# A graph-attention kernel on one Trainium2 core: gains ahead of rank weights, earlier statistics, split last tile, and half of the first gathers beside a fetch

## The chip, the cores and the metric

The kernel runs on one core of one Trainium2 chip. The metric is the time of one execution on the device, in microseconds (us). A core has a matrix engine (TensorE, PE in the profile, with its weight loads as PEld), a vector engine (VectorE, DVE), an activation engine (ScalarE, ACT), a general engine (GpSimd, POOL) and a queue engine that issues transfers (SyncE, SP). Each takes its instructions in the order in which the program gives them, and waits for the others by semaphores. SBUF is the on-chip memory; PSUM holds what TensorE writes.

## The reference

Each of 32 images x[b] has 512 channels and 1024 nodes. Two layers follow each other; each adds its input to its output and normalises over the nodes.

```python
# layer 0: attention over the nodes, in float32
q = jnp.einsum('c,bcn->bn', wq, x)
k = jnp.einsum('c,bcn->bn', wk, x)
scores = q[:, None, :] + k[:, :, None]
scores = jnp.where(scores > 0, scores, 0.01 * scores)
att = jax.nn.softmax(scores, axis=-1)
agg = jnp.einsum('bcn,bmn->bcm', x, att)
out = jax.nn.relu(jnp.einsum('oc,bcm->bom', adj, agg) + bm[None, :, None])
x = layernorm(x + out, axis=-1)
# layer 1: a masked product
W = adj * adj
x = layernorm(x + jnp.einsum('bnf,nm->bmf', x, W) + bias, axis=-1)
```

## The kernel before

**The method.** A score is a leaky ReLU of q[n] + k[m]. Above the threshold its exponential is a product of a factor of n and a factor of m, and below it another such product. So if the nodes are sorted by q, the attention of row m is a prefix sum up to a rank plus a sum from that rank on. The kernel never forms the 1024 x 1024 matrix. For an image b it goes through these stages, which are helper functions:

- `project` (L213): TensorE makes z = x^T [wq, adj^T, wk] for 128 nodes at a time (eight steps per image, each in two parts), and ScalarE copies it to `zrow` (L229).
- `spread`, `place`, `send` (L233 to L280): q is spread over all partitions, VectorE counts each node's rank (L262), and GpSimd scatters the rows of `zrow` to DRAM in rank order (L271), into one of two buffers `td` (image number modulo 2).
- `count` (L292): ScalarE counts, by a sign with an accumulated sum (L296), how many q lie above each node's threshold; `share` (L300) makes from it the index `idx` of the table row and a few exponentials.
- `fetch` (L317): SP reads the sorted rows back into the SBUF tile `zs`, in eight transfers, 2.1 MB. Columns 0, 1, 7 and 8 of its nine come first.
- `weigh` (L334): exponentials of q (ScalarE, L344) times a triangle (VectorE, L349) make the rank weights `lw`; part 0 covers the columns that come first, part 1 the rest.
- `table` (L356), nine steps per image: TensorE multiplies two columns of `zs` by the weights (L363), ScalarE copies the sums out of PSUM to `ts` (L368), the last sum is carried into the next columns (one row copied on GpSimd or VectorE, L372, and one on ScalarE, L374), and SP writes `ts` to `td` (L377). So each step waits for the one before it. There are two buffers for `ts` and one PSUM tile for all tables (pool `ps_t`).
- `pick` (L381): GpSimd gathers (L386), for 128 nodes at a time, three rows of the table (own row, sum from above, sum from below, 6 KB together) into the tile `g`; eight gathers per image, 6.3 MB. They wait until all nine steps of the image's table are in DRAM. `g` has one buffer for all images.
- `own`, `norm` (together `shares`, L395 to L425): the weights of those three rows, for four of the eight node blocks at a time. `scale` (ScalarE, L432) and `gain` (VectorE, two operations per block, L440) add the three rows up.
- `turn` (L474): TensorE turns the result round (L478), ScalarE applies bias and relu (L482). `join` (L485): VectorE adds x and takes the statistics (`stats`, L449, L451); `root` (GpSimd, L457, L458), `shift` (VectorE, L464) and `apply` (ScalarE, L470) normalise.
- `layer1` (L494): TensorE multiplies by W + I (L500); `stats1` (VectorE, L515, L449) takes the sum with the bias out of PSUM and its statistics; `root`, `shift`, `apply` normalise and `store` (L519) writes the tile out. An image has four such tiles `mt`. The pool `ps_mm` has three PSUM tiles of 128 x 1024, shared by all large products.

**The order.** The whole order of work is written by hand: an engine runs its instructions as the program emits them, and nothing is moved by a scheduler. `begin` (L549) projects images 0, 1 and 2 and makes the table of image 0; `opening` (L606) finishes layer 0 and most of layer 1 of image 0 and brings image 1 to its gains; `slot` (L649) runs for images 1 to 29 and overlaps four images; `end` (L732) has the last two images, 30 (`s`) and 31 (`mid`), and the last tiles of 29 (`old`). `last` (L522) is the very last output tile: it goes through PSUM in two halves so that VectorE can begin on the first.

In `begin`'s third loop (L573) TensorE projects image 2 while the remaining steps of image 0's table run; at z = 3 the sorted rows of image 1 are fetched, at z = 6 all eight gathers of image 0 are emitted behind step 0 of image 1's table, and steps 3 to 8 of that table follow in `opening`, with their carried rows copied by VectorE.

In `end`, image 30's layer 0 runs together with image 31's table: two steps ahead of the turns, four in the turns and three between the first matmuls of layer 1. Then the gathers of image 31 are issued and its gains follow, with the statistics of image 30's tiles 1 and 2 between them.

Of the kernel before, what the change touches and what calls it, by code (L numbers as in the profile page):

```python
# [8 lines left out]
F32 = mybir.dt.float32  # L9
# [14 lines left out]
def gat_gcn_resnorm_kernel(  # L24
# [38 lines left out]
    nc = tc.nc  # L63
# [222 lines left out]
    def top(b):  # L286

        qs, kc, sgn, qmax = info[b]
        nc.vector.tensor_reduce(qmax, qs, AX.X, ALU.max)
        nc.vector.tensor_scalar(bws[b], nel, qmax, None, ALU.mult)  # L290
# [200 lines left out]
        if ot > 0:  # L491
            apply(0, b, ot - 1)

    def layer1(b, mt, h, cts=range(CT)):  # L494

        yt = ys[b]
        if (b, mt) not in ops:
            ops[b, mt] = ps_mm.tile([P, N], F32, name=f"o1_{b}_{mt}", tag="mm")
        for ct in cts:
            nc.tensor.matmul(  # L500
                ops[b, mt][:, h * H : (h + 1) * H],
                w1[:, ct, mt * P : (mt + 1) * P],
                yt[ct][:, h * H : (h + 1) * H],
                start=(ct == 0),
                stop=(ct == CT - 1),
            )

    def layer1g(b, mts, ct):
        for mt in mts:
            for h in range(NH):  # L510
                layer1(b, mt, h, (ct,))
# [10 lines left out]
    def last(b, mt):  # L522

        t = vpool.tile([P, N], F32, name=f"v_{b}_{mt}", tag="v")
        st = small.tile([P, NH, 6], F32, name=f"st_1_{b}_{mt}", tag="st")
        mv = small.tile([P, 2], F32, name=f"mv_1_{b}_{mt}", tag="mv")
        halves = [slice(h * H, (h + 1) * H) for h in range(NH)]
        for h, some in enumerate(halves):
            layer1(b, mt, h)
            op = ops[b, mt]  # L530
            nc.vector.tensor_tensor(t[:, some], op[:, some], bias_bc[:, some], ALU.add)
            nc.vector.bn_stats(st[:, h, :], t[:, some])
            if h == 0:
                shift(1, b, mt - 1)
                apply(1, b, mt - 1)
                store(b, mt - 1)
        nc.vector.bn_aggr(mv, st)
        due[1, b, mt] = [t, mv]
        root(1, b, mt)
        shift(1, b, mt)  # L540
        t, mv, rs, nb = due.pop((1, b, mt))
        nc.scalar.activation(t[:, halves[0]], t[:, halves[0]], AF.Identity, bias=nb, scale=rs)
        nc.vector.tensor_scalar(
            t[:, halves[1]], t[:, halves[1]], rs, nb, ALU.mult, ALU.add
        )
        for some in halves:
            nc.sync.dma_start(out=out[b, mt * P : (mt + 1) * P, some], in_=t[:, some])

    def begin():  # L549


        for z in range(NT):
            project(0, z, 0)
            project(0, z, 1)
        spread(0)
        for nt in range(NT):
            order(0, nt)
        top(0)
        fetch(0)
        for z in range(NT):  # L560
            if z == NT - 2:
                weigh(0, 0)
            if z == NT - 1:
                weigh(0, 1)
            project(1, z, 0)
            if z == NT - 1:
                table(0, 0)
            project(1, z, 1)
            count(0, z)
        table(0, 1)  # L570
        share(0)
        spread(1)
        for z in range(NT):  # L573
            step = 2 * z + 2
            for nt in range(2 * z, 2 * z + 2):
                if nt < NT:
                    place(1, nt)
            project(2, z, 0)
            if step < NB:
                table(0, step)  # L580
            if z < NT // 2:
                send(1, 2 * z)
            project(2, z, 1)
            if step + 1 < NB:
                table(0, step + 1)
            if z < NT // 2:
                send(1, 2 * z + 1)
            if z == NT // 2 - 1:
                top(1)
                fetch(1)  # L590
            if z >= NT // 2 - 1:
                for nt in range(2 * z - 6, min(2 * z - 4, NT)):
                    count(1, nt)
            if z == NT - 3:
                weigh(1, 0)
            if z == NT - 2:
                table(1, 0)
                for mt in range(NT):
                    pick(0, mt)
                weigh(1, 1)  # L600
        table(1, 1, nc.vector)
        spread(2)
        table(1, 2, nc.vector)
        share(1)

    def opening():  # L606

        for step in (3, 4):
            table(1, step, nc.vector)
        shares(0, 0, NT // 2)  # L610
        for k in range(NT // 2):
            scale(0, [k])
            gain(0, [k])
            if k % 2:
                table(1, 5 + k // 2, nc.vector)
        shares(0, NT // 2, NT)
        for k in range(NT // 2, NT):
            scale(0, [k])
            gain(0, [k])
            if k % 2:  # L620
                table(1, 5 + k // 2, nc.vector)
        for ot in range(CT):
            turn(0, ot)
            join(0, ot)
            root(0, 0, ot)
            load(3, ot)
        shift(0, 0, CT - 1)
        apply(0, 0, CT - 1)
        for mt in range(NT):
            pick(1, mt)  # L630
        for nt in range(NT):
            order(2, nt)
            count(2, nt)
        top(2)
        fetch(2)
        for ct in range(CT):
            layer1g(0, range(CT - 1), ct)
        for mt in range(CT - 1):
            stats1(0, mt)
            root(1, 0, mt)  # L640
        for ct in range(CT):
            layer1g(0, (CT - 1,), ct)
        for mt in range(CT - 1):
            shift(1, 0, mt)
        shares(1, 0, NT // 2)
        scale(1, range(NT // 2))
        gain(1, range(NT // 2))
# [84 lines left out]
    def end():  # L732

        s, mid, old = B - 2, B - 1, B - 3
        for mt in range(CT - 1):
            apply(1, old, mt)
        shares(s, NT // 2, NT)
        scale(s, range(NT // 2, NT))
        weigh(mid, 0)
        gain(s, (4, 5))  # L740
        table(mid, 0)
        weigh(mid, 1)
        gain(s, (6, 7))
        table(mid, 1)
        stats1(old, CT - 1)
        root(1, old, CT - 1)
        for ot in range(CT):
            turn(s, ot)
            table(mid, 2 + ot)
            join(s, ot)  # L750
            root(0, s, ot)
            if ot == 0:
                shift(1, old, CT - 1)
                apply(1, old, CT - 1, by=nc.vector)
        share(mid)
        shift(0, s, CT - 1)
        apply(0, s, CT - 1)
        for mt in range(CT):
            store(old, mt)
        step = 2 + CT  # L760
        for ct in range(CT):
            for mt in range(CT - 1):
                layer1g(s, (mt,), ct)
                if step < NB:
                    table(mid, step)
                    step += 1
        for mt in range(NT):
            pick(mid, mt)
        stats1(s, 0)
        root(1, s, 0)  # L770
        for ct in range(CT):
            layer1g(s, (CT - 1,), ct)
        shares(mid, 0, NT // 2)
        scale(mid, range(NT // 2))
        gain(mid, (0, 1))
        own(mid, NT // 2, NT)
        gain(mid, (2, 3))
        norm(mid, NT // 2, NT)
        scale(mid, range(NT // 2, NT))
        shift(1, s, 0)  # L780
        apply(1, s, 0)
        stats1(s, 1)
        root(1, s, 1)
        gain(mid, (4, 5))
        stats1(s, 2)
        root(1, s, 2)
        gain(mid, (6, 7))
        for mt in (1, 2):
            shift(1, s, mt)
            apply(1, s, mt)  # L790
        for ot in range(CT):
            turn(mid, ot)
            join(mid, ot)
            root(0, mid, ot)
            if ot == 0:
                stats1(s, CT - 1)
                root(1, s, CT - 1)
        shift(0, mid, CT - 1)
        apply(0, mid, CT - 1)
        shift(1, s, CT - 1)  # L800
        apply(1, s, CT - 1)
        for mt in range(CT):
            store(s, mt)
        for ct in range(CT):
            layer1g(mid, range(CT - 1), ct)
        for mt in range(CT - 1):
            stats1(mid, mt)
            root(1, mid, mt)
            if mt > 0:
                shift(1, mid, mt - 1)  # L810
                apply(1, mid, mt - 1)
                store(mid, mt - 1)
        last(mid, CT - 1)
# [35 lines left out]
```

## Time and profile before

| what | us |
|---|---|
| median of 3 runs (lowest, highest) | 2413.76 (2410.81, 2415.1) |
| the profiled execution's own time | 2413.43 |
| its span, first to last instruction | 2411.7 |
| TensorE busy | 2302.5 |
| VectorE busy | 1672.2 |
| ScalarE busy | 1439.6 |
| GpSimd busy | 1022.5 |

A line of the page's table of slices gives one digit for each of 40 equal parts of the span (60.3 us each): tenths of busy time, or tenths of the full clock in the row PEclk. A timeline line gives start, duration, engine, source line, operation, output and inputs with their shapes, and in brackets the idle time before it and what ended it. The chain of waits that ended last goes through TensorE for 69% of the span; 7% each are VectorE and the issue of instructions, 6% GpSimd and 5% transfers.

### The profile page before, as it was taken

To read this page: it belongs to the slowest core of one execution; us is meant where nothing else is said; L and a number is where in the kernel's file an instruction comes from. 1 tells how busy PE (TensorE), PEld (TensorE's weight loads), DVE (VectorE), ACT (ScalarE), POOL (GpSimd) and SP (SyncE) were. 2 spreads that over 40 slices of the span, in tenths; PEclk is the share of its full clock that TensorE was granted. 3 is DMA by queue.
4 is the path that set the end of the run, shared out by engine and by line. 5 is a ranking of instruction groups with operands and counts; after the bars stand their busy time and mean duration, and the time that the engine had idled before them with its cause. 6 is when DMAs were issued, how large, how long until landed. Compare 5 with 4: busy or idle time off the path is not lost.

```text
span 2411.7 us, 30916 instructions
## 1 busy us (share of the span) xinstructions
PE 2302.5 (95%) x9744; PEld 1449.9 (60%) x9744; DVE 1672.2 (69%) x3490; ACT 1439.6 (60%) x2213; POOL 1022.5 (42%) x1284
## 2 busy tenths in 40 slices
PE   8968999999999999999999999999999999999776
PEld 7635655666666566666566666656665656666333
DVE  3266777776777776777777677767677776768655
ACT  2555655775665666655677565566665566656532
POOL 1233445433444533444543444453344454344431
PEclk9989999999999999999999999999999999999887
DMA  6566776767777766777676777676777767677641
GB/s 240 145 229 205 251 246 235 233 211 240 256 249 234 253 213 221 250 252 233 242 231 214 243 254 254 232 247 203 233 248 254 236 244 226 212 248 243 203 177 61
DMA packets 176835, 548.67 MB, mean 228 GB/s; under 512 B 26304, under 2 KB 26304, under 8 KB 176672
## 3 DMA queue, kind: packets, MB, share of 16 engines
q1 hardware_dynamic: 117600, 276.65, 38.8%
q0 software_dynamic: 57344, 269.52, 29.4%
q8 instruction: 77, 1.26, 0.2%
q14 instruction: 86, 0.70, 0.1%
q10 hardware_dynamic: 1728, 0.53, 0.1%
HBM read 338.17 MB, written 208.43 MB: 227 GB/s over the span
## 4 chain that ended last, share of the span: by engine, by line
PE 69%; DVE 7%; issue 7%; POOL 6%; DMA 5%; ACT 4%; SPq 0%; POOLq 0%; DVEq 0%; ACTq 0%
PE zp L221 29%; PE o L500 25%; PE tp L363 10%; DVE g L440 3%; PE op L478 3%; DMA g<-td,idx 3%; POOL td L271 2%; POOL zs L372 2%; ACT y L482 1%; DVE st L449 1%; PE qb L237 1%; POOL g L386 1%; POOL rs L458 1%; ACT ts L368 1%; ACT w L344 1%
## 5 line engine op out<-in xcount | busy, mean ns | idle before, releaser
L221 PE MATMUL zp<-wmT,x 128*128 128x257 f32 x4096 | 963.0, 386 | 3.6 <-ACT zrow L229 2.6
L500 PE MATMUL o<-y,adj_sb 128*128 128x512 f32 x2048 | 897.9, 596 | 11.1 <-ACT y L470 6.1
L221 PEld LDWEIGHTS zp<-wmT,x 128*128 128x128 f32 x4096 | 761.6, 191 | 200.5 <-issue 92.9
L500 PEld LDWEIGHTS o<-y,adj_sb 128*128 128x128 f32 x2048 | 385.3, 191 | 487.2 <-issue 468.9
L372 POOL COPY zs<-ts 1x513 f32<-1x513 f32 x249 | 200.4, 805 | 657.6 <-ACT ts L368 657.4
L440 DVE SCALAR_TENSOR_TENSOR g<-g,ra 128x512 f32<-128x512 f32 x512 | 369.9, 748 | 35.1 <-ACT g L432 26.0
L363 PE MATMUL tp<-zs,lw 128*64 128x257 f32 x2304 | 325.1, 401 | 45.0 <-POOL zs L372 19.0
L271 POOL DMA_INDIRECT td<-zrow,ranki x256 | 283.5, 1108 | 195.6 <-DVE ranki L266 124.1
L229 ACT COPY zrow<-zp 128x514 f32<-128x514 f32 x256 | 148.8, 581 | 323.7 <-PE zp L221 313.1
L262 DVE SCALAR_TENSOR_TENSOR lt<-qs,zrow,first 128x1024 int8<-128x1024 f32 x256 | 326.8, 1276 | 3.6 <-ACT qs L241 2.2
L386 POOL DMA_INDIRECT g<-td,idx x256 | 268.0, 1047 | 88.1 <-issue 82.7
L296 ACT ACTIVATE sg<-qs,kc 128x1024 int8<-128x1024 f32 x256 | 294.1, 1149 | 7.0
L489 DVE TENSOR_TENSOR y<-y,x 128x1024 f32<-128x1024 f32 x128 | 156.8, 1225 | 157.9 <-ACT y L482 156.2
L363 PEld LDWEIGHTS tp<-zs,lw 128*64 128x64 f32 x2304 | 150.5, 139 | 188.1 <-POOL zs L372 57.6
L457 POOL TENSOR_SCALAR rs<-mv 128x1 f32<-128x1 f32 x256 | 81.1, 317 | 416.7 <-ACT v L470 295.0
L368 ACT COPY ts<-tp 128x514 f32<-128x514 f32 x288 | 168.6, 585 | 113.4 <-PE tp L363 107.2
L408 ACT ACTIVATE ac<-s 128x4 f32<-128x4 f32 x64 | 13.3, 208 | 358.4 <-DVE s L407 180.1
L432 ACT ACTIVATE g<-g,ra 128x512 f32<-128x512 f32 x256 | 167.3, 713 | 57.7 <-DVE ra L419 36.9
L458 POOL TENSOR_TENSOR rs<-rs,mhalf 128x1 f32<-128x1 f32 x256 | 188.8, 738 | 21.3
L464 DVE SCALAR_TENSOR_TENSOR nb<-mv,rs 128x1 f32<-128x1 f32 x256 | 39.5, 156 | 218.9 <-POOL rs L458 218.9
L515 DVE TENSOR_TENSOR v<-o,bias_bc 128x1024 f32<-128x1024 f32 x127 | 154.7, 1218 | 28.3 <-PE o L500 28.1
L478 PE MATMUL op<-ident,g 128*128 128x128 f32 x1024 | 145.4, 285 | 29.3 <-DVE g L440 17.4
(75 smaller groups left out, 1628.4 us busy)
## 6 DMA issues: line engine op xcount, KB each, us to landing
x<-in_x_dram SPq DMA_DIRECT2D x128, 512.0 KB
out_dram<-v SPq DMA_DIRECT2D x127, 512.0 KB
td<-ts SPq DMA_DIRECT2D x512, 120.5 KB
zs<-td SPq DMA_DIRECT2D x64, 602.3 KB
zs<-td SPq DMA_DIRECT2D x64, 240.9 KB
zs<-td SPq DMA_DIRECT2D x96, 120.5 KB
td<-ts SPq DMA_DIRECT2D x64, 96.4 KB
td<-zs SPq DMA_DIRECT2D x8, 514.0 KB
```

The costliest lines, as they stand in the source:

```text
L221: nc.tensor.matmul(zp[:, h, 0:CE], xb[ct][:, nt * P : (nt + 1) * P], wmT[:, ct, h * CE : (h + 1) * CE], start=(ct == 0), stop=(ct == CT - 1),)
L262: nc.vector.scalar_tensor_tensor(lt, qs, zrow[:, nt, 0:1], first[:, o : o + N], ALU.subtract, ALU.is_lt, accum_out=rank[:, nt : nt + 1],)
L271: sc = nc.gpsimd.indirect_dma_start(out=td[:, :], out_offset=bass.IndirectOffsetOnAxis(ap=ranki[:, nt : nt + 1], axis=0), in_=zrow[:, nt, ...
L296: nc.scalar.activation(sg, qs, AF.Sign, bias=kc[:, nt : nt + 1], accum_out=sgn[:, nt : nt + 1])
L363: nc.tensor.matmul(tp[i * G : (i + 1) * G, h, 0:CE], lt[:, i, j, :], zs[:, j, h * CE : (h + 1) * CE], start=True, stop=True,)
L368: nc.scalar.copy(ts.rearrange("p (h c) -> p h c", h=2), tp[:, :, 0:CE])
L372: by.tensor_copy(zs[0:1, to, 1:ZW], ts[0:1, 1:ZW])
L386: nc.gpsimd.indirect_dma_start(out=gs[b][:, mt, :], out_offset=None, in_=tds[b].rearrange("(s u) c -> s (u c)", u=3), in_offset=bass.Indir ...
L440: nc.vector.scalar_tensor_tensor(u, g[:, k, i, 1 : C + 1], ra[:, k, i : i + 1], u, ALU.mult, ALU.add)
L458: nc.gpsimd.tensor_tensor(rs, rs, mhalf, ALU.pow)
L478: nc.tensor.transpose(op[:, mt * P : (mt + 1) * P], ub[mt][:, ot * P : (ot + 1) * P], ident)
L500: nc.tensor.matmul(ops[b, mt][:, h * H : (h + 1) * H], w1[:, ct, mt * P : (mt + 1) * P], yt[ct][:, h * H : (h + 1) * H], start=(ct == 0), ...
```

## The change

In `end`, image 30's second four gains come ahead of all of image 31's rank weights. All of image 31's table steps move two places later: four in the turns, five between the matmuls, and the second part of the weights follows the second step. The statistics of image 30's tiles 0, 1 and 2 come together behind the issue of image 31's gathers, and their applies ahead of image 31's shares. In `last`, the two halves get a PSUM tile each, one from `ps_t` and one from `ps_mm`, and all of the matmuls are emitted ahead of VectorE's work. In `begin`, four of image 0's eight gathers are emitted at z = 3, ahead of image 1's fetch; the weights and steps of image 1's table move one step of the loop earlier, with the other four gathers behind step 0. Step 2 goes ahead of image 2's spread. Steps 3 to 6 stay between the gains, their carried rows copied by GpSimd; steps 7 and 8 go to the turns, and `share` of image 1 comes between the gains.

```diff
@@ layer1
-    def layer1(b, mt, h, cts=range(CT)):
+    def layer1(b, mt, h, cts=range(CT), op=None):
-        if (b, mt) not in ops:
+        if op is not None:
+            ops[b, mt] = op
+        elif (b, mt) not in ops:
@@ last
+        ops_last = (
+            ps_t.tile([P, N], F32, name="last_0", tag="t"),
+            ps_mm.tile([P, N], F32, name="last_1", tag="mm"),
+        )
+        for h in range(NH):
+            layer1(b, mt, h, op=ops_last[h])
         for h, some in enumerate(halves):
-            layer1(b, mt, h)
-            op = ops[b, mt]
+            op = ops_last[h]
@@ begin
             if z == NT // 2 - 1:
+                for mt in range(NT // 2):
+                    pick(0, mt)
                 top(1)
                 fetch(1)
...
+            if z == NT - 4:
+                weigh(1, 0)
             if z == NT - 3:
-                weigh(1, 0)
-            if z == NT - 2:
                 table(1, 0)
-                for mt in range(NT):
+                for mt in range(NT // 2, NT):
                     pick(0, mt)
                 weigh(1, 1)
-        table(1, 1, nc.vector)
+            if z == NT - 2:
+                table(1, 1, nc.vector)
+        table(1, 2, nc.vector)
         spread(2)
-        table(1, 2, nc.vector)
-        share(1)
@@ opening
-        for step in (3, 4):
-            table(1, step, nc.vector)
         shares(0, 0, NT // 2)
         for k in range(NT // 2):
             scale(0, [k])
             gain(0, [k])
             if k % 2:
-                table(1, 5 + k // 2, nc.vector)
+                table(1, 3 + k // 2)
+        share(1)
         shares(0, NT // 2, NT)
         for k in range(NT // 2, NT):
             scale(0, [k])
             gain(0, [k])
             if k % 2:
-                table(1, 5 + k // 2, nc.vector)
+                table(1, 3 + k // 2)
         for ot in range(CT):
             turn(0, ot)
+            if ot < NB - 7:
+                table(1, 7 + ot)
             join(0, ot)
@@ end
         scale(s, range(NT // 2, NT))
+        gain(s, range(NT // 2, NT))
         weigh(mid, 0)
-        gain(s, (4, 5))
-        table(mid, 0)
-        weigh(mid, 1)
-        gain(s, (6, 7))
-        table(mid, 1)
         stats1(old, CT - 1)
         root(1, old, CT - 1)
         for ot in range(CT):
             turn(s, ot)
-            table(mid, 2 + ot)
+            table(mid, ot)
+            if ot == 1:
+                weigh(mid, 1)
             join(s, ot)
...
-        step = 2 + CT
+        step = CT
         for ct in range(CT):
             for mt in range(CT - 1):
                 layer1g(s, (mt,), ct)
...
         for mt in range(NT):
             pick(mid, mt)
-        stats1(s, 0)
-        root(1, s, 0)
+        for mt in range(CT - 1):
+            stats1(s, mt)
+            root(1, s, mt)
         for ct in range(CT):
             layer1g(s, (CT - 1,), ct)
+        for mt in range(CT - 1):
+            shift(1, s, mt)
+            apply(1, s, mt)
         shares(mid, 0, NT // 2)
         scale(mid, range(NT // 2))
         gain(mid, (0, 1))
...
         scale(mid, range(NT // 2, NT))
-        shift(1, s, 0)
-        apply(1, s, 0)
-        stats1(s, 1)
-        root(1, s, 1)
-        gain(mid, (4, 5))
-        stats1(s, 2)
-        root(1, s, 2)
-        gain(mid, (6, 7))
-        for mt in (1, 2):
-            shift(1, s, mt)
-            apply(1, s, mt)
+        gain(mid, range(NT // 2, NT))
```

## The prediction

> **What bounds the kernel now.** I read the table of slices first, then the chain that ended last at the start and at the end, then the timelines of each engine there.
>
> ```profile
> PE   8968999999999999999999999999999999999776
> PEclk9989999999999999999999999999999999999887
> ```
>
> TensorE is full in 34 of 40 slices, and the change leaves these slots alone: what they begin late or early is handed on unchanged. The holes are slices 3 (120 to 180 us) and the last three (2231 on). There the chain is one of waits, so a change is worth what it moves on that chain.
>
> The opening, ScalarE, GpSimd and VectorE in the timeline (start, duration, idle before and its releaser):
>
> ```profile
> 117.72 0.60 POOL L372 COPY zs<-ts 1x513 f32<-1x513 f32 x1 [13.82 <-ACT ts L368]
> 118.33 0.69 ACT L344 ACTIVATE w<-zs,bw,el 128x7 f32<-128x7 f32 x2
> 118.83 1.51 POOL L386 DMA_INDIRECT g<-td,idx  x1 [0.51 <-issue]
> 127.38 0.59 ACT L368 COPY ts<-tp 128x514 f32<-128x514 f32 x1 [2.38 <-DMA td<-ts]
> 130.93 0.59 ACT L368 COPY ts<-tp 128x514 f32<-128x514 f32 x1 [2.32 <-DMA td<-ts]
> 132.55 0.16 DVE L405 TENSOR_TENSOR s<-g,kc 128x4 f32<-128x4 f32 x1 [0.52 <-DMA g<-td,idx]
> ```
>
> GpSimd is idle 13.8 us before the eight gathers; VectorE then waits for their first half until 132.5. The fetch of image 1's rows was issued from 106.36 to 109.70. In windows of 2 us:
>
> ```profile
> 110.00:112.00 2.00, 2.00 (x11) 1.75 (x10) 0.00 (x0) 1.52 (x4) 0.00 (x0) 1.00 1.00 274
> 130.00:132.00 2.00, 0.32 (x2) 0.00 (x0) 0.38 (x1) 1.04 (x2) 0.00 (x0) 0.50 1.01 418
> ```
>
> The last two columns are DMA share and GB/s: the fetch alone fills the DMA engines at some 240 GB/s (2 KB packets), the gathers at some 420 (6 KB).
>
> The end:
>
> ```profile
> 2290.79 1.22 DVE L515 TENSOR_TENSOR v<-o,bias_bc 128x1024 f32<-128x1024 f32 x1
> 2316.02 0.59 ACT L368 COPY ts<-tp 128x514 f32<-128x514 f32 x1 [1.74 <-PE tp L363]
> 2328.18 1.22 DVE L515 TENSOR_TENSOR v<-o,bias_bc 128x1024 f32<-128x1024 f32 x1 [18.74 <-PE o L500]
> 2341.06 0.16 DVE L405 TENSOR_TENSOR s<-g,kc 128x4 f32<-128x4 f32 x1 [2.14 <-DMA g<-td,idx]
> 2356.51 2.37 ACT L470 ACTIVATE v<-v,nb,rs 128x1024 f32<-128x1024 f32 x2 [7.56 <-DVE nb L464]
> 2358.79 2.09 ACT L482 ACTIVATE y<-op,bm_sb 128x1024 f32<-128x1024 f32 x2
> 2395.57 5.35 PE L500 MATMUL o<-y,adj_sb 128*128 128x512 f32 x8 [2.14 <-DVE v L531]
> 2400.95 0.69 DVE L531 TENSOR_TENSOR v<-o,bias_bc 128x512 f32<-128x512 f32 x1 [4.65 <-PE o L500]
> ```
>
> VectorE is idle for 18.7 us up to 2328.18, and later does two older statistics between the gains; the two older applies stand on ScalarE ahead of the first relu (2358.79); the last half's matmuls wait 2.14 us for VectorE and then run at a low clock.
>
> [...] table 1's two writes (240 KB, ready at 121.1) landed at 127.4 under the gathers, table 2's at 130.9; 240 KB in the 3.5 us between is some 65 GB/s for the SP queue. [...] idle from 2338.4, the clock is at 0.5 by 2342; but the 2.14 us at 2393.4 were enough too (0.50 from 2396 to 2398). 8 table matmuls take 1.09 us warm and 2.0 cold.
>
> **The change part by part.** The order of each engine's instructions in the new program is known; durations are the trace's.
>
> *E1, gains ahead of rank weights.* ScalarE's four scales start at 2275.48 as before; eight gains of 0.735 follow each other to 2282.1 (before, the second four ended at 2290.87, behind the large weights product of 2286.45). Small product 0.57, older statistics 2.78: 2285.4. The first turn and relu are ready by 2283.8, so join 0 runs 2285.4 to 2288.2 (before from 2293.48). Table 0: TensorE 2.25 cold, copy 0.6, then GpSimd's zs copy, queued behind the older root (1.7), ends 2287.85. Table 1 and its ScalarE copies: 2291.2; weights part 1 0.69 and the product 1.16 now stand ahead of join 1: 2293.1, VectorE idle for 2.7 us. Joins 1 to 3 then go at the old beat of 4.0 (a root lies between): the last ends at 2304.0, its apply at 2306.4 (before 2310.7).
>
> *E2, five tables instead of three behind it.* Steps 4 to 8 lie between the matmuls; the copy of step 4 is queued behind that apply on ScalarE (to 2307.0). Each further step costs a table, 1.02, plus four matmuls, 1.91: 2.93. Steps 5 to 8 reach TensorE at 2307.65, 2310.6, 2313.5, 2316.5; the last copy ends at 2318.2, 1.6 later than now (2316.6). The gathers start at 2322.6 and land at 2335.0 and 2342.6 (now 2333.4, 2341.0). So 4.3 us won upstream become 1.6 lost here.
>
> *E3, older statistics in the hole.* With table 8 done at 2317.6, TensorE finishes the three tiles after five, six and seven more groups of four matmuls (1.74; 52 took 22.59): 2326.3, 2328.1 and 2329.9; three statistics of 2.7 end at 2334.5. Their roots wait on GpSimd behind the gathers' issue (to 2332.9): last root 2335.6. ScalarE applies three (3.5): 2338.3, and the exponent of the shares stands behind them, so the scales start at 2339.4, not 2335.2. Gains 0 to 3 with the second shares: to 2346.65; norm 0.7; a scale that is no longer hidden, 0.85; four pairs, 5.9: 2354.1. Now it is 2356.4, then 2.4 of applies. New: transpose 0.5, relu at 2354.7 against 2358.79: **4.05 won**. All behind it is the same chain (join 0, statistics 3, joins) to the last tile.
>
> *E4, last halves in own buffers.* The second half's 8 matmuls follow at once at the warm rate, 8 x 0.434 = 3.5, instead of 2.14 + 5.35. In old times VectorE can start the second half at 2396.95, not 2400.95; it is free at 2396.3. **4.0 won**; aggregate, root, applies, stores and the 6.2 from the last issue to the end stay. ps_t is free by then, and the mm buffer was read at 2387.8.
>
> *O, opening.* The first four gathers start when the last table's write has landed (about 105.8 and 1.2 of issue: 107), their data 2.4 later (as at 118.83: 121.2), at 109.4. By then the fetch has moved 0.4 of its 2.1 MB. The gathers' 3.16 MB take 10.5 us beside 65 GB/s of fetch: to 119.9. The fetch's first 0.74 MB then land at about 116 (now by 113.6), the rest, 1.0 MB at 240, at about 125.6 (now by 118.3). ScalarE waits from 110.2 for the first weights, with zrow copies and signs behind, and TensorE waits at table 0 (image 1), idle about 6 us. First table's copy at about 121; the second four gathers are queued behind it on GpSimd, 122.2 (now 124.6). ScalarE waits again for part 1: to 126.3; then zrow 0.5, two signs 2.6, table copy 0.6, zs copy 0.6, zrow 0.6, table 2 on TensorE 1.1, copies 1.2, qs 1.0, and only then the shares of image 0: 134.1, gains from about 136.2 (now 134.96). So although the gathered rows are there at 121, the chain runs through the fetch. The gains drop VectorE's zs copies (0.34 net each) and take the five small operations of share (0.9): nothing net. In the turns two tables are added before the second and third turn, 2.0 each cold; VectorE's joins (beat 3.9) cover them, barely. **Cost 1.2**, unknown from both sides: below, -4.5 if the fetch keeps half of the DMA engines (part 1 at 119.5); above, +5 if its tail meets the second gathers (0.3 MB at 65). I take 1.2 because table writes were just so slow under gathers.
>
> Sum against the profiled execution's own 2413.43 (span 2411.7, 1.7 around it): - 4.05 - 4.0 + 1.2 = -6.85: **2406.6**. The median of the runs, 2413.76, is 0.3 higher.
>
> **The rivals.** *Fetch unharmed:* the opening wins 4.5, total -12.5: 2400.9. For it: the fetch starts 3 us ahead. Against: the two late table writes. *Tail collision:* opening +5, total -3: 2410.4. For it: second gathers' data at 124.6 against the fetch's end at 124.1, half a microsecond apart. *Slower:* the fetch's tail is held until both sets of gathers are through, and with it image 1's table writes. 1.7 MB at 240 is 7.1, eight gathers at 430 are 14.7: from 109.4 to 131.2, and with start gaps and landing 135; part 1 is then 9.5 late, and tables that wait for their buffers' writes add 4: +13.5, total +5.5: 2418.9. It decides from a part 1 at about 133, where the end's 8 are used up. Against: a write did land under load in 6 us, not 12. That E1 does nothing is true in a sense (E2 gives it back), and is in the sum.
>
> **How the numbers follow.** Forecast 0.56 (own range 2404 to 2409), unharmed 0.16, collision 0.20, slower 0.08. The measurement tells 0.2%, 4.8 us, from no change: the line is 2408.9. Faster: 0.50 of the forecast and 0.16, 0.66; same: 0.06 and 0.20, 0.26; slower 0.08. Range 2401.0 to 2411.5: it reaches to the collision and to the edge of the unharmed case.
>
> **What would show it.** E4: no idle before the last 8 matmuls, about 3.5 us long. E3: three statistics before the shares, no apply just ahead of the first relu of the last image. E2: last table copy 1 to 2 us later. O: ScalarE waiting for zs twice between 110 and 126, first gains near 136. I am wrong if the weights of part 1 start before 122 or after 129, or if the gathers of the last image start after 2325.

## The result

The changed kernel takes 2405.19 us (median of 7 runs, 2403.2 to 2408.18) beside 2412.61 of the kernel before (7 runs taken with them, 2406.87 to 2417.57). The ratio is 0.9973, with a 95% interval of 0.9959 to 0.9986: 6.5 us less, between 3.4 and 9.9. The profiled execution of the changed kernel is the slowest of its seven, 2408.18, with a span of 2406.5 (before: 2413.43, span 2411.7): what it shows of single stretches is one draw, and further profiles are set beside it below.

Its page, TensorE and its clock in the 40 slices (now 60.2 us each):

```profile
PE   8778999999999999999999999999999999999876
PEclk9988999999999999999999999999999999999987
```

The holes are those of before, and slice 2 (60 to 120 us) has fallen from 9 to 7. To see which part gave what, the span is cut at four instructions that every version has. *Opening:* from SP's first fetch issue for image 1 (L324) to VectorE's first later copy of `qs` (L241), when the pipeline takes over. *Slots:* from there to the last copy of `qs`, 28 turns of the loop. *Hole:* from the second shares of image 30 (L405) to the first relu of image 31 (L482). *Tail:* from there to the end.

| us | opening | slots | hole | tail | span |
|---|---|---|---|---|---|
| before | 136.93 | 1998.35 | 84.97 | 52.91 | 2411.7 |
| after | 140.79 | 1994.64 | 83.83 | 48.20 | 2406.5 |
| difference | +3.9 | -3.7 | -1.1 | -4.7 | -5.2 |
| predicted | +1.2 | 0 | -4.05 | -4.0 | -6.85 |

(The four differences make -5.7; the other half microsecond lies ahead of, between and in the cuts.) So in these two profiles the total came out near, while of the four parts only the tail did.

**The opening.** The timeline of after (start, duration, in brackets the idle time before and its releaser):

```profile
107.26 1.05 POOL L386 DMA_INDIRECT g<-td,idx  x1 [2.47 <-DMA td<-ts]
120.42 0.67 ACT L344 ACTIVATE w<-zs,bw,el 128x2 f32<-128x2 f32 x2 [9.28 <-DMA zs<-td]
121.19 2.25 PE L363 MATMUL tp<-zs,lw 128*64 128x257 f32 x8 [9.61 <-DVE lw L349]
125.28 1.02 POOL L386 DMA_INDIRECT g<-td,idx  x1 [0.17 <-issue]
128.83 0.69 ACT L344 ACTIVATE w<-zs,bw,el 128x7 f32<-128x7 f32 x2 [3.74 <-DMA zs<-td]
138.89 6.47 DVE L440 SCALAR_TENSOR_TENSOR g<-g,ra 128x512 f32<-128x512 f32 x8 [0.79 <-ACT g L432]
```

The first four gathers are issued from 107.26, as early as the fetch (issued from 107.25). ScalarE waits 9.3 us for the fetch's first part and TensorE as long behind it; the second part arrives at 128.8, after the second gathers have been issued from 125.28. The gains begin at 138.89, 3.9 later than in the profile before; 0.9 of that is the later start of the fetch (107.25 for 106.36).

The chain of waits of after, and two windows (start and end in us, then busy time by engine, granted clock, DMA share, GB/s):

```profile
109.26 10.98 DMA zs<-td
```

```profile
112.00:114.00 2.00, 0.00 (x0) 0.00 (x0) 0.00 (x0) 0.00 (x0) 0.22 (x1) 1.00 1.03 259
124.00:126.00 2.00, 2.00 (x6) 1.63 (x5) 0.00 (x0) 1.06 (x2) 1.32 (x2) 0.50 0.98 209
```

From the last fetch issue the chain does nothing but wait for that fetch. In the first window the only busy time is 0.22 us of a gather's issue on GpSimd, and the DMA engines are full. In the second they are still full with the fetch's rest.

**The end.** The timeline of after:

```profile
2308.04 1.79 PE L363 MATMUL tp<-zs,lw 128*64 128x257 f32 x8 [2.94 <-POOL zs L372]
2309.76 2.93 PE L502 MATMUL o<-y,adj_sb 128*128 128x512 f32 x4
2312.62 1.09 PE L363 MATMUL tp<-zs,lw 128*64 128x257 f32 x8
2319.67 0.59 ACT L368 COPY ts<-tp 128x514 f32<-128x514 f32 x1 [1.70 <-PE tp L363]
2323.94 1.17 POOL L386 DMA_INDIRECT g<-td,idx  x1 [5.96 <-issue]
2333.20 0.99 POOL L386 DMA_INDIRECT g<-td,idx  x1 [0.30 <-issue]
2336.56 3.50 ACT L470 ACTIVATE v<-v,nb,rs 128x1024 f32<-128x1024 f32 x3 [16.30 <-DVE nb L464]
2337.83 2.59 SPq L522 DMA_DIRECT2D out_dram<-v  x3
2346.88 0.16 DVE L405 TENSOR_TENSOR s<-g,kc 128x4 f32<-128x4 f32 x1 [2.12 <-DMA g<-td,idx]
2358.30 1.12 ACT L482 ACTIVATE y<-op,bm_sb 128x1024 f32<-128x1024 f32 x1 [4.66 <-PE op L478]
2388.65 7.03 PE L502 MATMUL last<-y,adj_sb 128*128 128x512 f32 x16
2395.71 0.69 DVE L538 TENSOR_TENSOR v<-last,bias_bc 128x512 f32<-128x512 f32 x1 [0.61 <-PE last L502]
```

The timeline of before, its last gather's issue and its stores:

```profile
2330.24 0.99 POOL L386 DMA_INDIRECT g<-td,idx  x1 [0.30 <-issue]
2348.97 49.01 SPq L520 DMA_DIRECT2D out_dram<-v  x7
```

Three things are to be seen. The last table copy (2319.67) and with it the gathers are later. The three older applies start at 2336.56, and 1.3 us later SP issues three stores of finished tiles (before, the stores began at 2348.97); the gathers' second half lands at 2346.88, 13.7 us after the last gather's issue (before: 2330.24 to 2341.06, 10.8). And the last tile's 16 matmuls run without a gap, so VectorE takes its second half at once.

The DMA view of after, 2318 to 2350 (transfers issued, KB each, median us to landing):

```profile
out_dram<-v SPq DMA_DIRECT2D x3, 512.0 KB, 8.0
g<-td,idx POOLq DMA_INDIRECT x8, 9.0
```

### The profile page after: what moved, and what is told of

The parts are those of the page before. It is cut to its first block, busy times and chain, and to the rows that moved or that the text cites. A ratio compares the mean times of both kernels' runs of the same rounds, so it can differ in the third digit from the quotient of the medians.

```text
span 2406.5 us, 30937 instructions
## 1 busy us (share of the span) xinstructions
PE 2304.5 (96%) x9744; PEld 1450.5 (60%) x9744; DVE 1671.5 (69%) x3485; ACT 1440.2 (60%) x2213; POOL 1019.1 (42%) x1289
## 4 chain that ended last, share of the span: by engine, by line
PE 78%; DMA 5%; DVE 5%; ACT 4%; issue 4%; POOL 4%; SPq 0%; POOLq 0%; ACTq 0%; DVEq 0%
PE zp L221 32%; PE o L502 30%; PE tp L363 11%; PE op L478 3%; DVE g L440 3%; DMA g<-td,idx 3%; POOL zs L372 2%; ACT y L482 1%; PE qb L237 1%; ACT w L344 1%; DMA zs<-td 1%; ACT ts L368 1%; DVE st L449 1%; DMA td<-zrow,ranki 1%; POOL td L271 1%
## 5 line engine op out<-in xcount | busy, mean ns | idle before, releaser
L470 ACT ACTIVATE v<-v,nb,rs 128x1024 f32<-128x1024 f32 x126 | 154.8, 1231 | 33.0 <-DVE nb L464 33.0
## 6 DMA issues: line engine op xcount, KB each, us to landing
td<-ts SPq DMA_DIRECT2D x512, 120.5 KB, 2.2
zs<-td SPq DMA_DIRECT2D x96, 120.5 KB, 3.5
```

## The experiments

Each edit starts from the changed kernel unless it says otherwise; "one run" means that the time is that of the profiled execution alone, with the scatter of a single run.

**One part at a time.** `e1_opening_only` has `begin` and `opening` of the change, with `end` and `last` as before. `e2_end_only` is the reverse. `e3_last_only` changes `last` alone (the split of the last tile).

> Opening of the change alone, end as before. Theory A (four gathers beside the fetch starve it, and its tail then meets the second four): the stretch from the first fetch issue of image 1 to VectorE's first qs copy grows from 136.9 to about 140.8 us, so the kernel is 3 to 4 us slower than before. Rival B (the opening costs nothing on the whole because the 28 slots behind it run more evenly: they took 71.24 us on average in the changed kernel's profile, 71.37 in the old one's): the same stretch is 3.9 longer, but the time stays within 1 us of before.

> End of the change alone (with the split last tile), opening as before. Theory A (the parts add up: end -5.9 from the second shares of image 30 to the end of the span, slots by chance): 5 to 7 us faster than before, the stretch from the second shares of image 30 takes 132.0 us instead of 137.9. Rival B (a part of the gain comes from the slots behind the new opening): the same stretch, but only 2 to 4 us faster.

> Only the two PSUM tiles of the last output tile. Prediction's step E4: no idle before the last 8 matmuls, 4.0 us faster; the stretch from the first relu of image 31 to the end takes 48.2 instead of 52.9 us if all of the 4.7 that the tail lost belongs to the split, 48.9 if 4.0 do. Rival: VectorE, not TensorE, is the bound of the last tile (it is free only 0.65 us before), so that under 3 us come out.

| | time | ratio to before (95%) | opening | slots | hole | tail |
|---|---|---|---|---|---|---|
| e1 | 2412.95 | 1.0008 (0.9998 to 1.0017) | 140.59 | 1993.44 | 86.02 | 53.15 |
| e2 | 2403.21 | 0.9966 (0.9953 to 0.9980) | 138.31 | 1996.50 | 84.56 | 48.23 |
| e3 | 2407.3 | 0.9986 (0.9977 to 0.9995) | 136.84 | 1995.60 | 84.92 | 48.13 |

(kernel before beside them: 2410.87.) The new opening alone is no gain: its stretch is 3.7 longer, the slots are shorter, and the median of the runs is 2.1 longer, between the 3 to 4 of theory A and the 1 of its rival. The end alone is worth as much as the whole change, and the split alone takes 4.8 off the tail.

For E1 to E3 together, one profile and the runs disagree. The hole of e2 is only 0.4 shorter than that of before, but this profile is the slowest of e2's six runs (2407.55). By the medians e2, which has all of the end, is 4.1 us below e3, which has the split alone; the intervals of their ratios overlap only from 0.9977 to 0.9980. And over the profiles of all experiments, taken on several chips, the hole is 81.9 to 84.6 in the six with the end of the change (after, e2, e5, e7, e11, e12; mean 83.1) and 84.9 to 87.6 in the four with the old one (before, e1, e3, e6; mean 85.9). So E1 to E3 do win, some 3 to 4 us by these two comparisons; the 1.1 of the two profiles above lies low.

**How many gathers beside the fetch.** `e5_no_gather_beside` (one run) issues all eight behind table 0, as before, and leaves the rest of the new opening; `e7_two_gathers_beside` (one run) has two beside it. The diff is that of e7; e5 drops the first of these loops, and the second runs over range(NT).

```
             if z == NT // 2 - 1:
-                for mt in range(NT // 2):
+                for mt in range(2):
                     pick(0, mt)
...
-                for mt in range(NT // 2, NT):
+                for mt in range(2, NT):
                     pick(0, mt)
```

> The changed kernel, but all eight gathers of image 0 behind step 0 of image 1's table (still one loop step earlier than before), none beside the fetch. Theory A (the gathers slow the fetch, and image 1's weights hold everything up): first rank weights of image 1 on ScalarE about 6 us after the first fetch issue, not 13.2, second part by 12, not 21.6; the stretch from the first fetch issue to the first qs copy on VectorE falls from 140.8 to 136.5 or 137, as before the change. Rival E (the cost comes from the new order of tables, share and turns, whatever the fetch does): it stays at 140 or more.

> The changed kernel with two gathers of image 0 beside the fetch instead of four, six behind step 0. Theory A: the fetch is held back in proportion, second part of the weights 16 to 18 us after the first fetch issue (12 with none, 21.6 with four), and the stretch to the first qs copy between 137 and 139.5. Rival E: 140 or more.

The weights of both parts in the timelines of e5 and, below, e7:

```profile
112.02 0.67 ACT L344 ACTIVATE w<-zs,bw,el 128x2 f32<-128x2 f32 x2 [2.56 <-DMA zs<-td]
118.12 0.69 ACT L344 ACTIVATE w<-zs,bw,el 128x7 f32<-128x7 f32 x2 [1.42 <-DMA zs<-td]
```

```profile
119.49 0.67 ACT L344 ACTIVATE w<-zs,bw,el 128x2 f32<-128x2 f32 x2 [7.26 <-DMA zs<-td]
125.71 0.69 ACT L344 ACTIVATE w<-zs,bw,el 128x7 f32<-128x7 f32 x2 [1.55 <-DMA zs<-td]
```

The landing of the fetch's two large transfers, which come last and carry its second part, from the DMA views 106 to 130 of e5, e7 and after:

```profile
zs<-td SPq DMA_DIRECT2D x2, 602.3 KB, 7.0
```

```profile
zs<-td SPq DMA_DIRECT2D x2, 602.3 KB, 11.7
```

```profile
zs<-td SPq DMA_DIRECT2D x2, 602.3 KB, 16.2
```

Every two gathers (1.6 MB) put some 4.5 us on it. The opening stretch is 136.62 with none and 136.84 with two (137 to 139.5 was expected). With four it is 140.79, and 140.59 to 142.72 in the five profiles that share this opening (after, e1, e4, e9, e12). Two therefore cost nothing that can be seen and gain nothing either; four cost 4 to 6. Times: 2401.34 and 2403.52 beside 2410.15 of the kernel before on that chip.

**When the stores go.** `e4_stores_later` leaves every computation in place and puts the store of tile 3, which is finished last, ahead of the other three in SP's order:

```
         apply(1, s, CT - 1)
-        for mt in range(CT):
+        for mt in (CT - 1, 0, 1, 2):
             store(s, mt)
```

> The changed kernel, with image 30's store of tile 3 emitted ahead of those of tiles 0 to 2, so that SP holds these three (1.5 MB) back until about 2378. Theory C (the early applies release three stores into the last image's gathers): the second half of the gathers lands 10.8 us after the last gather's issue as before the change, not 13.2, and the first relu of image 31 comes 2 to 2.4 us earlier; the stores that now run late may take up to 1 us of it back at the last tile's buffers. Rival D (the gathers themselves are slower because of where they fall among other transfers): 13 us still, no gain.

The timeline of e4, last gather's issue, second shares and first relu:

```profile
2329.61 0.99 POOL L386 DMA_INDIRECT g<-td,idx  x1 [0.30 <-issue]
2341.07 0.16 DVE L405 TENSOR_TENSOR s<-g,kc 128x4 f32<-128x4 f32 x1
2352.47 1.11 ACT L482 ACTIVATE y<-op,bm_sb 128x1024 f32<-128x1024 f32 x1 [4.66 <-PE op L478]
```

The shares now come 11.5 us after the last issue instead of 13.7, and the hole is 80.67 instead of 83.83; 0.9 of these 3.2 is that the gathers were issued 0.9 earlier after the second shares of image 30, which the order of the stores does not explain. Nothing but the order of four transfers differs. One execution scatters, so the lag from the last gather's issue to the shares is compared over all runs. With the stores among the gathers it is 13.7 (after), 12.6 (e12 below, the same kernel), 13.5 (e2), 12.9 (e5 and e7) and 13.7 (e11). Without them it is 10.8 (before), 11.2 (e1), 10.9 (e3), 11.5 (e4), 11.0 (e6 and e9), 11.4 (e8) and 11.8 (e10); in e4 and e10 VectorE comes to the shares without having waited, so the landing can be earlier still. The two groups do not overlap, and their means are 2 us apart (13.2 and 11.2): the three stores do hold the gathers up.

The tail is 0.9 longer (49.13). The timelines of after and, below, e4 have the whole of it in the 48 matmuls ahead of the last tile:

```profile
2366.25 22.56 PE L502 MATMUL o<-y,adj_sb 128*128 128x512 f32 x48 [3.04 <-ACT y L470]
```

```profile
2360.42 23.55 PE L502 MATMUL o<-y,adj_sb 128*128 128x512 f32 x48 [3.75 <-ACT y L470]
```

They take 23.28 in e12 too, where the stores go early, so the late stores are not shown to cost anything. The time is 2403.42, ratio 0.9974 (0.9966 to 0.9982), about that of the change: the shorter hole is not seen in the whole, and the opening of e4, which is that of the change, took 1.9 longer in its profile (142.72).

**Applies held back.** `e9_held_applies` (one run) keeps the three statistics early but puts the three applies, which the stores wait for, behind the last scales. `e8_old_tables_held_applies` (one run) does so in e2, with the old order of gains and tables (two tables ahead of the turns, three behind).

```
-        for mt in range(CT - 1):
-            shift(1, s, mt)
-            apply(1, s, mt)
         shares(mid, 0, NT // 2)
...
         scale(mid, range(NT // 2, NT))
+        for mt in range(CT - 1):
+            shift(1, s, mt)
+            apply(1, s, mt)
         gain(mid, range(NT // 2, NT))
```

> Opening and table order of the end as before (two steps ahead of the turns, rank weights ahead of the gains); from the change the early statistics and the split last tile are kept; the three early applies, and with them the stores, stand behind the last image's second scales. Theory C (five tables behind the turns and the released stores each cost what the gathers' landing shows, 2.4 to 3.0 and 2.4): gathers issued 47.1 us after the second shares of image 30 and landed 10.8 after the last issue, so the first relu of image 31 at 78.8 instead of 83.8 (before 85.0), and the end stretch 127 us instead of 132.0 (before 137.9). Rival D (VectorE and ScalarE between gathers and relu bind, not the landing): relu not under 82.

> The changed kernel with its three early applies (and so the stores that they release) moved behind the last image's second scales; table order as changed. It parts the two costs in the end. Theory C: the gathers are issued as late as in the changed kernel (48.5 to 49.5 us after the second shares of image 30), but land 11 after the last issue instead of 13.7; the first relu of image 31 at 81.4 or less (changed 83.8, with the old table order too 80.3). If the table order alone costs what the issue shows, 0.5 to 1.5 us more than 80.3 remain. Rival D: 83 or more.

The timeline of e9:

```profile
2333.52 0.99 POOL L386 DMA_INDIRECT g<-td,idx  x1 [0.30 <-issue]
2344.51 0.16 DVE L405 TENSOR_TENSOR s<-g,kc 128x4 f32<-128x4 f32 x1 [2.12 <-DMA g<-td,idx]
2351.16 3.49 ACT L470 ACTIVATE v<-v,nb,rs 128x1024 f32<-128x1024 f32 x3
2352.41 2.60 SPq L522 DMA_DIRECT2D out_dram<-v  x3
2355.91 1.11 ACT L482 ACTIVATE y<-op,bm_sb 128x1024 f32<-128x1024 f32 x1 [1.26 <-PE op L478]
```

The landing is back at 11.0 us, the stores go when nothing else moves, and the applies fit ahead of the relu, which waits for TensorE anyway. The hole is 81.08 in e9, as theory C expected, and 80.33 in e8, where 78.8 was expected. The first gather was issued 49.4 us after image 30's second shares in e9, as in the changed kernel (49.5). In e8, with the old tables, it was issued after 48.3 (47.1 before and expected), and the first half's shares then waited for the three statistics. Times: 2405.62 (before beside it: 2411.91) and 2402.51 (2410.15).

**Together.** `e10_no_gather_old_tables_held` has e5's opening, and in `end` the old order of tables and gains with the early statistics, the held applies and the split last tile.

> What the runs so far have as the best of each part: the changed opening without gathers beside the fetch, the old table order in the end, early statistics with held applies, split last tile. If the stretches add up: opening 136.6 us, slots 1994.5, end 128.4, which is 2397 to 2399 us, 12 to 14 us (0.5 to 0.6%) faster than before and 6 to 8 faster than the changed kernel. Rival: the slots lose again what the opening wins (1997 or more), 9 to 10 us faster than before.

The timeline of e10:

```profile
2324.21 0.99 POOL L386 DMA_INDIRECT g<-td,idx  x1 [0.30 <-issue]
2335.99 0.16 DVE L405 TENSOR_TENSOR s<-g,kc 128x4 f32<-128x4 f32 x1
2347.39 1.12 ACT L482 ACTIVATE y<-op,bm_sb 128x1024 f32<-128x1024 f32 x1 [1.26 <-PE op L478]
```

2398.51 us against 2411.91, ratio 0.9946 (0.9929 to 0.9963): twice the gain of the change, with two of its parts (E1 with E2, and the gathers beside the fetch) taken out. Its hole is 78.42, the shortest of all; VectorE goes from the first gains to the second shares (2335.99) without an idle time, so here it no longer waits for the gathers' landing. The time is as expected (2397 to 2399), its parts less so: the slots took 1996.55 instead of 1994.5, the end 126.6 instead of 128.4.

**The slots.** 28 turns at 71.08, the shortest turn seen, are 1990.2; single turns lose 0.1 to 1.7 more. A theory was that the count of small instructions on VectorE and GpSimd shifts this loss, as the new opening copies carried rows on GpSimd. `e6_rows_by_gpsimd` (from before) gives these copies to GpSimd, `e11_rows_by_vector` (from the change) back to VectorE, and `e12_changed_again` is the changed kernel unaltered (one run each).

In e6, and likewise for steps 2 to 8:

```
-        table(1, 1, nc.vector)
+        table(1, 1)
```

In e11, in both loops over the gains, and likewise for `table(1, 7 + ot)`:

```
-                table(1, 3 + k // 2)
+                table(1, 3 + k // 2, nc.vector)
```

> The kernel before, with the seven carried rows of image 1's table copied by GpSimd in place of VectorE, as the changed opening does for four more of them. Question: the 28 slots took 1992.7 to 1994.6 us in the three profiles with the new opening and 1995.6 to 1998.4 in the three with the old one, and the slot at 1100 to 1172 us lost 0.8 to 1.0 only with the old one. Theory F (where the instruction streams of VectorE and GpSimd stand in the slots decides, so that a few instructions more or less upstream move such losses): the slots come out at 1992 to 1995 and that slot loses nothing. Rival G (the new order of the opening's transfers or its later start does it): 1995.5 or more, and that slot still loses 0.8 to 1.0.

> The changed kernel with image 1's carried rows copied by VectorE throughout, as before the change, so that VectorE and GpSimd run as many instructions ahead of the slots as in the kernel before. Theory F (the place of the instruction streams in the slots decides what the slots lose): slots 1995.5 to 1998.5 us, as with the old opening. Rival G (the order of the opening's work, not the number of instructions): 1992.5 to 1994.7, as in the five profiles with the new opening.

> The changed kernel once more, unaltered, for one more profile: how far do the stretches of one and the same kernel differ between executions? If the slots' total is a matter of chance, it may lie anywhere from 1992.7 to 1998.4 us, where the other profiles lie; if the program decides it, within 0.5 of 1994.6. The opening's stretch (140.8) and the end's (132.0) should come out within 1.5 either way, since waits and transfers set them.

| | opening | slots | hole | time (before beside it) |
|---|---|---|---|---|
| e6 | 143.99 | 1995.88 | 87.58 | 2422.13 (2410.15) |
| e11 | 142.67 | 1997.18 | 84.21 | 2410.68 (2411.91) |
| e12 | 140.89 | 1993.99 | 81.89 | 2404.99 (2410.04) |

e11 lost the slots' gain, as the theory had it, but e6 did not win it (1992 to 1995 was expected), and e10, which copies on GpSimd too, has 1996.55. Nor is a late start simply absorbed: in e5 and e7 the opening is as short as before and the slots still take 1994.46, while e6 has the longest opening and an ordinary 1995.88. Kernels with the same opening as before scatter from 1995.60 to 1998.35, those with the new opening and four gathers beside the fetch (e11 apart) from 1992.70 to 1994.64. The gain of some 3 us goes with the new opening in seven of the nine profiles that have it in some form; its cause stays open. e12 also shows what one profile is worth: same kernel, slots 0.65 apart, hole 81.89 instead of 83.83, because its gathers were issued 0.9 earlier and landed in 12.65 instead of 13.7.

## Why the prediction was right, by its steps

*O, the opening: mis-sized.* +1.2 was forecast, +3.9 came (3.0 up to the first gains, counted from the fetch's first issue, and 0.8 behind them). The mechanism was right: the chain runs through the fetch, ScalarE waits for `zs` twice. Counted from the first fetch issue, its parts were to be used at 9.6 and 19.2 us and were used at 13.2 and 21.6. The failed term is the first: it was 3.6 too small, while the second part came 8.4 behind the first and not 9.6. The DMA queues of after from 109.40 to 120.42 (packets, MB, share; q0 has the gathers, q1 the fetch):

```profile
q0 software_dynamic: 432, 2.42, 68.0%
q1 hardware_dynamic: 525, 0.96, 32.1%
```

So the fetch was not slower than the 65 GB/s taken from the table writes; it moved at 87, beside gathers at 220 (the forecast, 3.16 MB in 10.5 us, has 300 for them). What failed is the amount. The forecast lets the first part land when 0.74 MB of the fetch have moved. That leaves out the rows of column 8 (two transfers, 120.5 and 8.0 KB, 0.13 MB), and the first part does not land ahead of all the rest: from 107.00 on, 1.14 MB of the fetch had moved when ScalarE used it at 120.42, and in e5, with no gathers beside it, 1.19 MB as well. The 0.4 MB more would take 4.6 us at 87 GB/s (an estimate from these figures).

The rival *tail collision* had the price (+5) nearer than the forecast, but its mechanism is a small part here: of the second gathers, 0.27 MB had moved by 128.83, when the second part was used. In e4, e9 and e12 it was 0.57 to 0.72 MB and the second part was used at 22.6 to 23.4 us, so there it may have counted; no run parts this out. e7 shows that the price is a matter of dose and vanishes at two gathers. A smaller term was also missed: four gains with GpSimd copying rows beside them take 6.47 us (after, e5, e12), where eight operations at the earlier rate would take 5.96. Of the marks by which the prediction would have called itself wrong, two were only just not reached: part 1 at 128.83 (after 129), the last image's gathers at 2323.94 (after 2325).

By the landings of the fetch's large transfers (7.0, 11.7 and 16.2 us in e5, e7 and after), the queue of 2 KB packets fell behind by some 4.5 us for each 1.6 MB that the queue of 6 KB rows had beside it, though its transfers were issued at the same time (107.25 and 107.26 in after). In the stretch above the two queues had 525 and 432 packets (100 of all these are under 512 bytes). By what rule the DMA engines divide their time between the two no run here shows; the half for the fetch, on which the forecast's lower case (-4.5) rests, was the author's assumption, and the share measured in this stretch is 32.1%.

*E1, gains first: right.* Join 0 was forecast at 2285.4 and began at 2285.79, and the last apply ended at 2306.85 (forecast 2306.4), though the stretch began 0.65 later than before.

*E2, five tables behind it: mis-sized.* The last table copy was to be 1.6 later and is 3.0 later, counted from image 30's second shares (45.2 after 42.2; in the eight profiles with this order 44.3 to 45.7, with the old one 41.5 to 43.1, and 45.3 in e6). The failed term is "each further step 2.93", priced at the full clock. TensorE stood idle for 2.94 us ahead of step 5 and came back slow: 1.79 and 2.93 us for the table and its four matmuls, where the next ones, from 2312.62 at a granted clock of 1.00, take 1.09 and 1.98, so 1.65 more. The clock granted at step 5 is the third figure from the end:

```profile
2308.00:2310.00 2.00, 1.96 (x9) 0.93 (x10) 0.00 (x0) 0.13 (x1) 0.00 (x0) 0.57 0.41 123
```

The prediction had read off the profile before that the clock was at 0.50 from 2396 to 2398, behind 2.14 us of idleness. It did not apply this to step 5, where 2.94 us went ahead of the 0.57.

*E3, older statistics in the hole: a wait left out.* The statistics did lie in the hole and the relu no longer stands behind applies, but "4.05 won" became 1.1 in this profile. (The forecast's own times, 2358.79 and 2354.7, make 4.09.) What was left out is the queue behind the moved instruction: a store waits for its apply, so moving three applies also moved three stores, 1.5 MB, from a quiet time into the gathers of the last image. In this profile the gathers landed 2.9 later, in the mean of all profiles 2.0, and e4 and e9 show that the stores were the cause. Of the 3.6 us by which the relu missed its forecast (2358.30 for 2354.7), 2.9 are this, 0.7 the late issue of E2 and 0.65 the later start of the stretch, less 0.7: in the forecast VectorE reached the second shares half a microsecond after their landing, and the work behind them was a little quicker.

*E4, split last tile: right, a little small.* -4.7 for -4.0, and -4.8 alone in e3. The idle 2.14 and the slow 5.35 are gone as worked out; the rest was not followed up.

*The total.* In the two profiles it came out by errors that cancelled: O lost 2.7 more and E1 to E3 won 2.9 less than forecast, E4 won 0.7 more, and the slots gave 3.7 that no step foresaw. The medians of the runs put the parts nearer to the forecast: the opening alone cost 2.1 (+1.2 forecast), E1 to E3 won 4.1 between e3 and e2 (4.05), and the split alone won 3.6 (4.0). How much of the agreement is luck can't be told from this. It is luck in part, since the forecast knew neither the 2 us that the stores cost nor the shorter slots.

## What to carry to other kernels

When an instruction is moved, follow what is queued behind its result: an apply that comes sooner lets its store go sooner, and a finished tile's store is easily sent at a bad time (here three stores of 512 KB put some 2 us on the gathers' landing). A transfer that the chain needs next should not share the DMA engines with one that is needed later unless the dose is small; try a half of it (here two gathers beside the fetch cost nothing that could be seen, four cost 4 to 6 us). Work put behind a wait of TensorE is priced at the clock which that wait leaves (here 0.57 after 2.94 us, so 1.65 us more for one table and four matmuls).

## What the runs showed of the hardware

- Three 512 KB stores beside eight gathers of 0.79 MB put some 2 us on the gathers' landing (13.2 for 11.2 us in the mean of six and eight profiles, 2.9 in the profile of after), though the gathers were issued first (in after from 2323.94 to 2333.20, the stores from 2337.83).
- A fetch of 2 KB packets beside gathers of 6 KB rows moved at 87 GB/s and the gathers at 220 (after, 109.40 to 120.42). Its first part was usable only when some 1.15 MB of the fetch had moved (1.14 in after, 1.19 in e5), though that part is 0.87 MB.
- After an idle time of 2.94 us TensorE came back at a granted clock of 0.57 (after, 2308 to 2310), and a table took 1.79 us for the 1.09 of the next one, at 1.00.
- Row copies of 0.6 us given to GpSimd queue behind its gathers' issue: in e6 the second copy ran behind eight issues of 1.3 us each, at 129.89 (on VectorE in before: 121.16), and the opening became 7 us longer (143.99 for 136.93). Eight operations of VectorE's gains took 6.47 us with the copies on GpSimd (after, e1, e5, e9, e10, e12; in e4 and e7 once 6.60 and 6.62), and 2.99 and 2.97 for each four with the copies on VectorE (before, e8, e11).
